# Attention's residual sum on TensorE and ScalarE, its statistics and the fusion moved to other half slots

## The chip, the cores and the metric

The kernel runs on one core of one Trainium2 chip. The metric is the device time of one execution in microseconds; lower is better. All data is float32.

## The reference, cut to what matters

The input is x, 8 samples of 512 channels by 48 x 48 = 2304 positions. Two layers follow, each with its input normalized over groups of 16 channels (`_gn`), and each with its input added to its output.

```
x = x + attention(_gn(x))      # causal linear attention, 8 heads of 64
x = x + mamba4(_gn(x))         # four 128-channel blocks in a chain

attention: q, k, v = 1x1 projections; Q = elu(q)+1; K = elu(k)+1
  out[l] = (sum_{j<=l} (Q[l].K[j]) V[j]) / (Q[l] . sum_{j<=l} K[j])

mamba4, for block i = 0..3:
  x_i = x[:, block i] + fused_{i-1}                 # fused_{-1} = 0
  xs, z = conv and silu of x_i @ Wi;  dt, B, C = xs @ Wx
  h_t = exp(delta_t A) h_{t-1} + delta_t xs_t B_t    # 256 channels x 16 states
  x_m = ((sum_n C_t h_t) + xs D) * silu(z) @ Wo
  fused_i = w_local * x_i + w_global * max(x_i, x_m) # weights from means over positions
```

The layer's output is the four `fused_i`. The statistics of the second `_gn` are taken of the first layer's output, x plus attention.

## The kernel before, in words

**Tiles.** Channels lie on the 128 partitions. The 2304 positions are cut into NC = 6 pieces of LC = 384. A **job** is one piece of one mamba block of one sample: 8 x 4 x 6 = 192 jobs. A **chunk** is one piece of attention for 128 output channels (two heads) of one sample: also 192. Samples are dealt to two streams, and the jobs of both are interleaved by a fixed list of turns; within a stream the jobs follow the chain of blocks.

**Slots and halves.** A job has SLOTS = 8 slots, each with four scans of 128 x 384 (`scan`, L830, on DVE). Order is written out by hand: `slot(k)` issues the product of B and the scaled input for the next slot (`product`, L809, on DVE), the work of other tasks for the first half (`beside(2k)`), two scans, the rest of a product two slots ahead (`last_product`, L798, POOL), the tasks of the second half (`beside(2k + 1)`), and two more scans. Then `weigh` (L846, POOL) multiplies by C, and one slot and a half later `gather` (L853, PE) sums the states into the PSUM tile `yp`. So each job has 16 halves, 0 to 15. Nothing reorders the instructions later: each engine works through its own in the order of issue, and waits by semaphores.

**Decays.** Before each scan ACT computes its decay, exp of 128 x 385 (`decay`, L819), into one of six PSUM banks. Up to three decays are issued ahead (five around the table loads), as far as banks are spare. A scan gives its bank back. All projections and small matmuls take their banks from the same six.

**Tasks.** Chunks, preparations of jobs and the fusion are generators. A `yield` names the half from which the next stage may be issued, and how many banks it needs. A chunk starts at `times[m]`, a multiple of 16 halves plus 3 in most cases. So its stage `at(j)` comes in half (3 + j) mod 16 of a job: the two projections' relu operations in halves 4 and 6, the mask product (L434) in half 8, the output matmuls `ops` (L443, L447, stage 22) in half 9, the sum with the input `xr` (L450, stage 24) and its statistics (L452) in half 11, and in the last chunk of six the group norm's steps from stage 28 on (half 15). The input tile `xr` is loaded anew in stage 18 (L424, half 5); it has one buffer. `save` notes a store, which `flush` issues on SP's queue two halves later or more.

**Preparation of a job** (`prepare`, with `first` the half of its own first scan): the convolution is issued at `first - 21` and `first - 19` (halves 11 and 13; L635), the silu operations with their table loads at `first - 18` (half 14, slot 7; L671 to L676), the copy of dbc (L687) in half 0, and the softplus with its table loads (L706) around half 2; then the two products of delta on POOL (L747), and loads for the scans from `first - 7` on, all on SP's queue.

**Fusion** (`pass_on`) turns the old block's piece in `xi` into the new block's input. For pieces 1 to 5 it loads three tiles (`loads`: xb, fu, xo) at `first - 36`, then from `first - 30` on, half by half, come three ACT operations (L596, L597, L601, in half 2), and three POOL operations: fu (L604), xi (L609) and xo (L612), followed by the store of xo to the output. Piece 0 is done as soon as the block before is finished. The job's convolution reads `xi`; a job may begin when its stream's `ready` exceeds its piece.

Of the kernel before, what the change touches and what calls it, by code (L numbers as in the profile page):

```python
# [49 lines left out]
def attention_then_mamba_kernel(  # L50
# [17 lines left out]
    nc = tc.nc  # L68
    B, _, L = x.shape
# [16 lines left out]
    ident = cst[:, C_ID : C_ID + P]  # L86
# [67 lines left out]
    def save(out, in_):  # L154
        stores.append((half_no[0], out, in_))

    def flush(every=True):
        while stores and (every or stores[0][0] <= half_no[0] - 2):
            _, o, i = stores.pop(0)
            nc.sync.dma_start(out=o, in_=i)  # L160
# [46 lines left out]
    norms, xns, x1s, done, ksums = {}, {}, {}, {}, {}  # L207
# [58 lines left out]
    def chunk(m):  # L266


        b, o, c = parts[m]
        n = f"{b}_{o}_{c}"  # L270
        bank = Banks()
        NT = LC // T
        cols, tile_rows = slice(c * LC, (c + 1) * LC), slice(o * P, (o + 1) * P)
        subs = [slice(i * T, (i + 1) * T) for i in range(NT)]
        heads_of = [slice(par * 64, par * 64 + 64) for par in range(2)]

        def at(j, gap=1):
            return times[m] + j, gap

        def new(tag, bufs=1, shape=(P, LC)):  # L280
            return apool.tile(list(shape), F32, tag=tag, name=f"{tag}_{n}", bufs=bufs)
# [50 lines left out]
        S, stats, ksum = passes[b, o]  # L332
# [9 lines left out]
        q = new("q", 2)  # L342
# [39 lines left out]
        kl, v = new("kl", 1, (P, NT, P)), new("v", 2, (P, NT, P))  # L382
# [20 lines left out]
        place = range(NT + 1) if c % 2 == 0 else range(NT, -1, -1)  # L403
# [19 lines left out]
        xr = new("xr")  # L423
# [8 lines left out]
        for par, sc in enumerate(scs):  # L432
            sm = new(f"sm{par}", 1, (P, NT, T))
# [2 lines left out]
        bank.free(2)  # L436
        yield at(22), 1
        ops = bank()[:, 0:LC]
        for i in range(NT):
            old = c > 0 or i > 0  # L440
            for h, sm in zip(heads_of, sms):
                if old:
                    nc.tensor.matmul(  # L443
                        ops[h, subs[i]], S[h, place[i], :], q[h, subs[i]], start=True, stop=False
                    )
            for h, sm in zip(heads_of, sms):
                nc.tensor.matmul(ops[h, subs[i]], v[:, i, h], sm[:, i, :], start=not old, stop=True)  # L447
        read[0] = m + 1
        yield at(24), 0
        nc.vector.tensor_add(xr, xr, ops)  # L450
        bank.free()
        nc.vector.bn_stats(stats[:, 0, c, :], xr)  # L452
        save(x1s[b][tile_rows, cols], xr)
        if c + 1 == NC:
            norm = yield from group_norm(
                stats, 1, f"m{b}_{o}", 8, [(times[m] + j, 1) for j in (28, 29, 29, 30, 31)]
            )
            flush()
            done[b, o] = norm

    class Stream:
# [62 lines left out]
        def pass_on(self):  # L524


            xi = self.xi
            old = None
            if self.b is not None:
                old = self.b, self.s, self.n, self.fm  # L530
                wt = small.tile([P, 4], F32, tag="wt", name=f"wt_{self.n}")
                nc.vector.tensor_copy(wt[:, 2:3], self.sums)
                nc.vector.tensor_reduce(wt[:, 3:4], self.fsum, AX.X, ALU.add)
            last = old is not None and old[1] == 3 and not self.samples
            if not last:
                self.move_on()
                while (self.b, self.s) not in done:
                    yield "1w", 0
                norm = done[self.b, self.s]
            s = self.s  # L540
            if old is not None:
                yield "1", 0

                nc.scalar.activation(wt[:, 0:2], wt[:, 2:4], AF.Exp, scale=-1.0 / L)
                yield "1", 0
                nc.vector.tensor_scalar_add(wt[:, 0:2], wt[:, 0:2], 1.0)
                nc.vector.reciprocal(wt[:, 0:2], wt[:, 0:2])
            else:
                yield "1", 0
            if not last:  # L550
                if self.fresh:
                    self.sums = norm[:, 2, :]
                else:

                    sums = small.tile([P, 2], F32, tag="sums", name=f"sums_{self.n}", bufs=3)
                    nc.vector.tensor_scalar(
                        sums[:, 0:1], wt[:, 2:3], wt[:, 0:1], norm[:, 2, :], ALU.mult, ALU.add
                    )
                    nc.vector.tensor_scalar(
                        sums[:, 1:2], wt[:, 3:4], wt[:, 1:2], sums[:, 0:1], ALU.mult, ALU.add  # L560
                    )
                    self.sums = sums[:, 1:2]

            def loads(c):
                fu = xb = xa = None
                cols = slice(c * LC, (c + 1) * LC)
                if not last:
                    xb = mpool.tile([P, LC], F32, tag="xb", name=f"xb_{self.n}_{c}")
                    nc.sync.dma_start(out=xb, in_=x1s[self.b][s * P : (s + 1) * P, cols])
                if old is not None:  # L570
                    fu = mpool.tile([P, LC], F32, tag="fu", name=f"fu_{old[2]}_{c}")
                    nc.sync.dma_start(out=fu, in_=old[3][:, cols])
                    xa = mpool.tile([P, LC], F32, tag="xo", name=f"xo_{old[2]}_{c}")
                    nc.sync.dma_start(out=xa, in_=x1s[old[0]][old[1] * P : (old[1] + 1) * P, cols])
                return fu, xb, xa

            now = loads(0)
            for c in range(NC):

                if c and not last:  # L580
                    first = 2 * self.jobs[self.block * NC + c].start
                    yield (first - 36, 1), 0
                    now = loads(c)
                    yield (first - 30, 1), 0
                elif c:
                    yield "3", 0
                    now = loads(c)
                    yield "1", 0
                else:
                    yield "1", 0  # L590
                cols, icols = slice(c * LC, (c + 1) * LC), slice(3 + c * LC, 3 + (c + 1) * LC)
                fu, xb, xa = now
                if not last:
                    normed = dict(bias=norm[:, 1, :], scale=norm[:, 0, :])
                if old is not None:
                    nc.scalar.activation(fu, fu, AF.Copy, scale=wt[:, 1:2])  # L596
                    nc.scalar.activation(xi[:, icols], xi[:, icols], AF.Copy, scale=wt[:, 0:1])  # L597
                if old is None:
                    nc.scalar.activation(xi[:, icols], xb, AF.Identity, **normed)
                elif not last and not self.fresh:  # L600
                    nc.scalar.activation(xb, xb, AF.Identity, **normed)  # L601
                if old is not None:
                    yield "1", 0
                    nc.gpsimd.tensor_tensor(fu, fu, xi[:, icols], ALU.add)  # L604
                    yield "1", 0
                    if not last and self.fresh:
                        nc.scalar.activation(xi[:, icols], xb, AF.Identity, **normed)
                    elif not last:
                        nc.gpsimd.tensor_tensor(xi[:, icols], xb, fu, ALU.add)  # L609
                    self.ready = c + 1  # L610
                    yield "1", 0
                    nc.gpsimd.tensor_tensor(xa, xa, fu, ALU.add)  # L612
                    save(out[old[0], old[1] * P : (old[1] + 1) * P, cols], xa)
                self.ready = c + 1
# [335 lines left out]
    parts, times = [], []  # L950
# [17 lines left out]
    for b in counted:  # L968
        first = times[parts.index((b, 0, 0))]
        begins[b] = (first - 20) // PERIOD * PERIOD - 4 * NC * PERIOD - 2 if b > 1 else first - 64  # L970

    def begin(latest):

        nonlocal begun, put
        while counted and begins[counted[0]] - 4 <= half_no[0]:
            tasks.append(Task(statistics(counted.pop(0))))
        while put < len(parts) and times[put] - 6 <= half_no[0]:
            put += 1
            heads.append(Task(chunk(put - 1), before=heads[-1] if heads else None))
        while (  # L980
            begun < len(jobs)
            and jobs[begun].start <= latest
            and jobs[begun].stream.block == jobs[begun].block
            and jobs[begun].stream.ready > jobs[begun].c
        ):
            tasks.append(Task(jobs[begun].prepare(), jobs[begun].start))
            begun += 1
# [41 lines left out]
    def at(k):  # L1029
        return jobs[k // SLOTS], k % SLOTS  # L1030
# [170 lines left out]
```

## Time and profile before

| | |
|---|---|
| three runs | 9154.76 us median (9140.69 to 9157.51) |
| profiled execution | 9167.14 us |
| its span, first to last instruction | 9165.3 us |
| instructions | 120476 |
| granted TensorE clock, mean | 0.961 |
| busy: DVE, POOL, PE, ACT | 8342.1, 8066.8, 7631.5, 6579.4 us |
| first scan; from the last job's first scan to the end | at 232.2 us; 83.4 us |
| data moved by DMA | 1642.84 MB, mean 179 GB/s; queue 1 takes 65.0% of 16 engines |

How to read it: a line of the groups view gives source line, engine, operation, output from inputs, shape and count, then the group's busy time, the mean duration of one in ns, and the engine's idle time right before its instructions with who ended it. A line of the waits view gives who waited for whom, the total in us, the times and the longest. A line of the timeline gives the start, the duration, engine, line, operation, tiles and how many instructions are merged in it; idle time before the first is in brackets. PE is matmuls and PEld weight loads. A float32 matmul of this kernel appears as two matmul records. Matmul ends are modelled, so PE's busy time is above what the array needs.

### The profile page before, as it was taken

What the parts mean: (1) busy time and instruction counts of PE and PEld (TensorE: products, weight loads), DVE (VectorE), ACT (ScalarE), POOL (GpSimd) and SP (SyncE); (2) the same over time, 40 slices, a digit from 0 to 9 for tenths busy, and PEclk for the clock granted to TensorE, in tenths of its full rate; (3) what the DMA queues carried; (4) which work ended last, traced back from release to release, by engine and by line L of the source; (5) the groups of instructions that cost most, each with busy time, mean ns of one, the idle gap of its engine ahead of it and who ended that gap; (6) DMA issues with size and microseconds to landing.
All of it is one profiled execution on the core that took longest, in us unless ns stands there. A gap on an engine that the chain in (4) does not pass through costs nothing.

```text
span 9165.3 us, 120476 instructions
## 1 busy us (share of the span) xinstructions
PE 7631.5 (83%) x35714; PEld 3602.8 (39%) x35714; DVE 8342.1 (91%) x11640; ACT 6579.4 (72%) x12656; POOL 8066.8 (88%) x5635
## 2 busy tenths in 40 slices
PE   7888888888888888888888888888888888888865
PEld 4443444433344444443333444444333444444321
DVE  3899999999999999999999999999999999999997
ACT  2677777777777777777777777777777777777775
POOL 1788989899988899899998888998999898989998
PEclk9999999999999999999999999999999999999977
DMA  5566666666766666666666666666666666666654
GB/s 182 161 173 180 185 184 184 181 188 180 196 173 179 184 186 187 183 180 181 191 184 182 174 178 187 187 184 184 180 188 183 181 179 177 178 178 177 164 156 129
DMA packets 1002898, 1642.84 MB, mean 179 GB/s; under 512 B 138592, under 2 KB 797312, under 8 KB 1002240
## 3 DMA queue, kind: packets, MB, share of 16 engines
q1 hardware_dynamic: 1002240, 1635.13, 65.0%
q8 instruction: 283, 4.64, 0.2%
q14 instruction: 375, 3.07, 0.1%
HBM read 1309.06 MB, written 325.58 MB: 178 GB/s over the span
## 4 chain that ended last, share of the span: by engine, by line
DVE 31%; ACT 21%; PE 18%; POOL 10%; DMA 9%; issue 8%; SPq 3%; POOLq 0%; DVEq 0%; ACTq 0%
DVE u L830 20%; ACT bank L819 7%; PE bank L635 6%; POOL u L846 6%; DVE u L809 6%; PE bank L286 5%; ACT L819 4%; PE yp L853 3%; PE bank L646 3%; POOL u L798 2%; DMA C<-scr 2%; ACT L706 2%; ACT bank L299 1%; DMA B<-scr 1%; SPq L739 1%
## 5 line engine op out<-in xcount | busy, mean ns | idle before, releaser
L830 DVE TENSOR_TENSOR_SCAN u<-bank,u 128x385 f32<-128x385 f32 (+1 forms) x6144 | 5471.0, 939 | 378.3 <-ACT bank L819 331.9
L846 POOL TENSOR_TENSOR u<-u,C 128x1536 f32<-128x1536 f32 x1536 | 4880.6, 3177 | 216.4 <-DVE gm_m L175 83.2
L819 ACT ACTIVATE bank<-dr,av 128x385 f32<-128x385 f32 (+1 forms) x6144 | 3432.3, 579 | 1406.9 <-DVE u L830 1118.1
L853 PE MATMUL yp<-u,cst 128*64 128x384 f32 x12288 | 2429.2, 516 | 505.7 <-ACT yp L787 263.9
L798 POOL TENSOR_TENSOR u<-B,dxr 128x512 f32<-128x512 f32 x1536 | 1958.8, 1275 | 21.4 <-DMA dxr<-xscr 16.9
L809 DVE TENSOR_TENSOR u<-B,dxp 128x1024 f32<-128x1024 f32 x1536 | 1835.0, 1195 | 9.4 <-ACT dxp L782 9.4
L286 PE MATMUL bank<-xn,wq_sb 128*128 128x384 f32 x4608 | 1730.3, 520 | 97.1 <-DVE u L830 40.4
L853 PEld LDWEIGHTS yp<-u,cst 128*64 128x64 f32 x12288 | 781.0, 139 | 1713.3 <-issue 1051.6
L635 PE MATMUL bank<-xi,wk 128*128 128x384 f32 x3072 | 1122.1, 509 | 306.1 <-ACT kl L383 234.3
L286 PEld LDWEIGHTS bank<-xn,wq_sb 128*128 128x128 f32 x4608 | 870.0, 199 | 894.6 <-DVE u L830 153.6
L635 PEld LDWEIGHTS bank<-xi,wk 128*128 128x128 f32 x3072 | 563.0, 193 | 878.2 <-ACT kl L383 351.5
L844 POOL COPY state<-u 128x4 f32<-128x4 f32 x1280 | 241.7, 189 | 538.4 <-DVE u L830 522.7
L298 ACT ACTIVATE ex<-bank,bqkv_sb 128x384 f32<-128x384 f32 x384 | 219.6, 572 | 520.1 <-PE bank L286 491.6
L747 POOL TENSOR_TENSOR delta<-delta,xs 128x384 f32<-128x384 f32 x384 | 384.6, 1002 | 141.6 <-DMA dscr<-delta 124.6
L819 ACT ACT_TABLE_LOAD x382 | 490.1, 1283 | 6.7
L787 ACT ACTIVATE yp<-xs,pv 128x384 f32<-128x384 f32 x384 | 222.7, 580 | 373.2 <-DVE yz L865 373.2
L871 PE MATMUL bank<-yz,wo 128*128 128x384 f32 x768 | 307.0, 517 | 55.5 <-DVE yz L865 36.7
L695 PE MATMUL bank<-dbc,wd 9*128 9x384 f32 x768 | 302.2, 513 | 3.2 <-ACT dbc L687 3.2
L646 PE MATMUL bank<-xi,wi 128*128 128x384 f32 x768 | 289.2, 498 | 14.3 <-ACT xs L671 14.3
L416 PE MATMUL bank<-cst,rdb 128*128 128x128 f32 x576 | 103.2, 290 | 228.3 <-DVE u L830 226.1
L447 PE MATMUL bank<-sm,v 128*64 128x128 f32 x2304 | 260.9, 305 | 33.8 <-DVE u L830 30.6
L682 PE MATMUL bank<-xs,wx 128*40 128x384 f32 x768 | 281.3, 489 | 0.8 <-DVE sm L434 0.8
(109 smaller groups left out, 7632.7 us busy)
## 6 DMA issues: line engine op xcount, KB each, us to landing
B<-scr SPq DMA_DIRECT2D x1536, 192.0 KB
C<-scr SPq DMA_DIRECT2D x1536, 192.0 KB
xn<-xn SPq DMA_DIRECT2D x192, 768.0 KB
dr<-dscr SPq DMA_DIRECT2D x768, 192.0 KB
dxr<-xscr SPq DMA_DIRECT2D x768, 192.0 KB
dscr<-delta SPq DMA_DIRECT2D x192, 384.0 KB
xscr<-delta SPq DMA_DIRECT2D x192, 384.0 KB
xn<-in_x SPq DMA_DIRECT2D x48, 768.0 KB
```

The lines of the kernel that those rows point to most:

```text
L286: nc.tensor.matmul(ps, wq_sb[:, kt, j * 512 + o * P : j * 512 + (o + 1) * P], xn[:, kt, :], start=(kt == 0), stop=(kt == 3),)
L635: nc.tensor.matmul(xc, wk[:, k, h * P : (h + 1) * P], xi[:, c0 + k : c0 + k + LC], start=(k == 0), stop=(k == 3),)
L646: nc.tensor.matmul(zp, wi[:, 256 + h * P : 256 + (h + 1) * P], xi[:, c0 + 3 : c0 + 3 + LC], start=True, stop=True,)
L695: nc.tensor.matmul(vp, wd[32:41, h * P : (h + 1) * P], dbc[32:41, :], start=True, stop=True)
L747: nc.gpsimd.tensor_tensor(delta[:, h, :], delta[:, h, :], xs[:, h, :], ALU.mult)
L798: nc.gpsimd.tensor_tensor(u[:, :, :, 1 + LC - TAIL :], self.B[s % 4][:, :, cols].unsqueeze(2).to_broadcast(shape), self.dxr[s // 4][:, :, ...
L809: nc.vector.tensor_mul(u[:, :, :, 1 : 1 + LC - TAIL], self.B[s % 4][:, :, cols].unsqueeze(2).to_broadcast(shape), self.dxp.unsqueeze(1).to ...
L819: nc.scalar.activation(dA[:, cols], self.dr[h][:, g, cols], AF.Exp, scale=self.w[6][:, 2 * h + g, q + j : q + j + 1],)
L830: nc.vector.tensor_tensor_scan(u[:, j, g, cols], dA[:, cols], u[:, j, g, cols], 0.0, ALU.mult, ALU.add,)
L846: nc.gpsimd.tensor_tensor(h, h, self.C[s % 4].unsqueeze(2).to_broadcast([P, NG, 2, LC]), ALU.mult)
L853: nc.tensor.matmul(self.yp[g * 64 : g * 64 + 64, 0:LC], pair_sum, u[:, j, g, 1:], start=False, stop=(s % 4 == 3 and j == NG - 1), skip_gro ...
L871: nc.tensor.matmul(self.xm[:, 0:LC], self.w[2][:, h, :], self.yz[:, h, :], start=(h == 0), stop=(h == 1),)
```

## The change

Three things are changed. First, `xr` is put into the bank of `ops` by a matmul with the identity, the attention's own matmuls are added to it in place (none of them starts the bank any more), and ACT copies the bank to `xr`, where DVE added the two. Second, the statistics of `xr` are taken in stage 28 in place of 24, after the store has been noted; the group norm's steps follow with at least one half between them, the last from stage 32. Third, the fusion of pieces 1 to 5 loads at `first - 33` and computes from `first - 25` on. In halves of a job: statistics 11 to 15, fusion's loads 12 to 15, its ACT operations 2 to 7, its POOL operations 3, 4, 5 to 8, 9, 10.

```diff
         ops = bank()[:, 0:LC]
+        nc.tensor.matmul(ops, ident, xr, start=True, stop=False, skip_group_check=True)
         for i in range(NT):
             old = c > 0 or i > 0
             for h, sm in zip(heads_of, sms):
                 if old:
                     nc.tensor.matmul(
-                        ops[h, subs[i]], S[h, place[i], :], q[h, subs[i]], start=True, stop=False
+                        ops[h, subs[i]],
+                        S[h, place[i], :],
+                        q[h, subs[i]],
+                        start=False,
+                        stop=False,
+                        skip_group_check=True,
                     )
             for h, sm in zip(heads_of, sms):
-                nc.tensor.matmul(ops[h, subs[i]], v[:, i, h], sm[:, i, :], start=not old, stop=True)
+                nc.tensor.matmul(
+                    ops[h, subs[i]],
+                    v[:, i, h],
+                    sm[:, i, :],
+                    start=False,
+                    stop=i == NT - 1,
+                    skip_group_check=True,
+                )
         read[0] = m + 1
         yield at(24), 0
-        nc.vector.tensor_add(xr, xr, ops)
+        nc.scalar.copy(xr, ops)
         bank.free()
+        save(x1s[b][tile_rows, cols], xr)
+        yield at(28), 0
         nc.vector.bn_stats(stats[:, 0, c, :], xr)
-        save(x1s[b][tile_rows, cols], xr)
         if c + 1 == NC:
             norm = yield from group_norm(
-                stats, 1, f"m{b}_{o}", 8, [(times[m] + j, 1) for j in (28, 29, 29, 30, 31)]
+                stats, 1, f"m{b}_{o}", 8, [(times[m] + j, 1) for j in (28, 29, 29, 30, 32)]
             )
...
                 if c and not last:
                     first = 2 * self.jobs[self.block * NC + c].start
-                    yield (first - 36, 1), 0
+                    yield (first - 33, 1), 0
                     now = loads(c)
-                    yield (first - 30, 1), 0
+                    yield (first - 25, 1), 0
```

## The prediction

> **What bounds the kernel now.** First the page's busy line:
>
> ```profile
> PE 7631.5 (83%) x35714; PEld 3602.8 (39%) x35714; DVE 8342.1 (91%) x11640; ACT 6579.4 (72%) x12656; POOL 8066.8 (88%) x5635
> ```
>
> DVE is nearest to full, POOL close behind. So ask what fills DVE's other 9%. The waits view (who waited for whom: total, times, longest):
>
> ```profile
> ACT bank L819 <- DVE u L830: 1118.1, 1807, 3.3
> ...
> DVE u L830 <- ACT bank L819: 331.9, 198, 4.4
> ...
> DVE k L351 <- ACT bank L299: 142.0, 135, 5.3
> ...
> DVE norm_m L195 <- POOL norm_m L191: 43.4, 31, 2.2
> ...
> DVE xr L450 <- PE bank L447: 40.2, 16, 8.8
> ```
>
> Most of the time ACT waits for DVE, but 198 times, about once in each of the 192 jobs, a scan waits for its decay, and 135 times k waits for ACT's relu. To place them I counted the scans in the timeline (32 to a job) and laid jobs 12 to 187 over each other: a job takes 46.34 us, of which DVE idles 3.20: 1.58 before the last scan of slot 7, 0.71 before k (slot 3), 0.28 before the norm factors, 0.21 before the first scan of slot 2, 0.09 before the add; the remaining 0.33 is scattered.
>
> The groups view, shapes apart, prices the parts (busy, mean ns, idle before):
>
> ```profile
> L596 ACT ACTIVATE fu<-fu,wt 128x384 f32<-128x384 f32 x192 | 117.0, 609 | 47.8 <-DMA fu<-fm 46.5 <-DVE wt L547 1.2
> ...
> L452 DVE BATCH_NORM_STATS2 stats_m<-xr 128x6 f32<-128x384 f32 x192 | 107.6, 560 | 6.6
> ...
> L450 DVE TENSOR_TENSOR xr<-xr,bank 128x384 f32<-128x384 f32 x192 | 101.4, 528 | 40.2 <-PE bank L447 40.2
> ...
> L384 ACT COPY v<-bank 128x384 f32<-128x384 f32 x192 | 92.8, 483 | 0.0
> ```
>
> Now one job whose first scan starts at 1020.70. ACT's timeline, then PE's, then DVE's:
>
> ```profile
> 1025.19 0.61 ACT L596 ACTIVATE fu<-fu,wt 128x384 f32<-128x384 f32 x1
> 1025.71 0.60 ACT L597 ACTIVATE xi<-xi,wt 128x384 f32<-128x384 f32 x1
> 1026.21 0.69 ACT L601 ACTIVATE xb<-xb,norm_m 128x384 f32<-128x384 f32 x1
> 1026.81 0.57 ACT L819 ACTIVATE bank<-dr,av 128x385 f32<-128x385 f32 x1
> 1027.39 1.28 ACT L706 ACT_TABLE_LOAD   x1
> ...
> 1033.43 0.57 ACT L787 ACTIVATE yp<-xs,pv 128x384 f32<-128x384 f32 x1
> ```
> ```profile
> 1034.15 1.92 PE L853 MATMUL yp<-u,cst 128*64 128x384 f32 x8 [1.99 <-ACT yp L787]
> 1036.00 4.08 PE L286 MATMUL bank<-xn,wq_sb 128*128 128x384 f32 x8
> ```
> ```profile
> 1041.18 0.56 DVE L351 SCALAR_TENSOR_TENSOR k<-ex,bank 128x384 f32<-128x384 f32 x1 [1.89 <-ACT bank L299]
> ```
>
> Fusion stands ahead of the softplus work and its two table loads; the skip into yp comes out late, PE waits 1.99 us for it, its k projection takes 4.08 us (2.85 elsewhere, for example at 1042.32), relu follows, and DVE's k is 1.89 late. The 4.08 is TensorE's clock, as the windows view shows over the same stretch of the job before (mean 1.00, k only 0.15 late) and this one (0.66); PEclk is the third figure from the end:
>
> ```profile
> 988.00:993.50 5.50, 4.64 (x22) 2.43 (x24) 5.50 (x10) 3.57 (x8) 5.50 (x6) 1.00 0.20 71
> 1034.00:1039.00 5.00, 4.85 (x14) 2.32 (x15) 5.00 (x8) 2.64 (x7) 4.92 (x7) 0.66 0.22 84
> ```
>
> The second big stall is the silu slot: from 1061.48 ACT runs a table load, four silus and a load back, and DVE gets its next decay only here:
>
> ```profile
> 1066.78 2.66 DVE L830 TENSOR_TENSOR_SCAN u<-bank,u 128x385 f32<-128x385 f32 x3 [1.11 <-ACT bank L819]
> ```
>
> **What the Trainium skill says.** "TensorE: Matmul & The Clock Gate", Part 1: an idle PE falls to half clock, judged in free-running windows of about 3.4 us. The 0.66 agrees; but its rule of avoiding gaps above some 3 us is too mild here, where 1.99 us was enough (and 1.90 in the job before was not). "ScalarE: Activation LUTs", What ACT_TABLE_LOAD costs: a load is about 1283 ns, and the trace has 1283; the drain of 1380 ns that it adds is not seen (1027.39 + 1.28, next start 1028.69). "PSUM — Partial Sum Buffer", The four PSUM rules: only the first matmul of a group resets a bank, the rest add; so opening the bank with x times identity needs no clearing instruction. No run here shows that yet.
>
> **The change, part by part** (us over the run, negative is a gain).
>
> 1. The add leaves DVE: 192 x 528 ns = -101. DVE is the busiest engine, so it counts in full. Its 40.2 of waits for PE are 16 early ones; in jobs 12 to 187 nearly none at the median: I take 0.
> 2. TensorE gets 192 matmuls of 128x384 by the identity. Eight matmul records (four such products) take 2.85 us, so one is 0.71: +137 on PE, none on the path. PE sits idle 7.35 us per job, among it 1.50 at 1056.58 waiting for pr, right behind the lengthened stretch. It must wait for the load of xr: SP issues that 8.8 us (5th percentile) to 17 us ahead of these matmuls, and loads that something waited for took 2 to 10 us to land. Bounds 0 to +40; I take 0.
> 3. ACT gets 192 copies from PSUM, as `v`: 192 x 483 ns = +93 on ACT, none on the path: behind it in slots 5 to 7 ACT waits 1.87 + 0.72 + 0.25 us per job for DVE before the silu work begins. A late PE would hold up the decays queued behind the copy; three decays ahead (3 x 0.94 us of scans) cover that.
> 4. bn_stats goes from slot 5 to before the third scan of slot 7, inside the silu stall. 560 ns against a mean of 1.58 there (one job in 48 has under 0.56): -107 from slot 5, about +7 where it does not fit: -100. What is late next is the same decay, by 1.0 us instead of 1.58.
> 5. Fusion's three ACT operations (1.9 us of durations, about 1.7 as they overlap) leave half 2 for half 7. Yp comes up to 1.6 us earlier (then the q projection, which ended near 1030.8 in this job, and its two ACT operations set it), PE's pause goes from 1.99 to about 0.4, half clock there becomes rare, and k's wait goes: -142 to 0; I take -110. The first scan of slot 2 waits for a decay behind the second table load, 0.21 x 176 = 37: I take -25. In half 7 ACT waited 0.53 + 0.27 + 0.80 us for DVE afterwards, which takes in most of 1.7: 0 to +30, I take 0.
> 6. Fusion's POOL operations (3 x 1.0) go from halves 3, 4, 5, where they stood against the two delta products (2 x 1.0, halves 5, 6), to 8, 9, 10. POOL's start of `weigh` lags the scans by 2.35 us at the median in slot 2 and 5.5 at the 95th percentile; that shrinks. Its three loads move on SP from half 12 to 15, with 8 halves to use instead of 6, behind B2 and C0 and ahead of B3 of the next job; the out store moves from before xscr to before B2, and SP now waits for it there. SP waited 1277 us for dbc and 968 for delta, so it has slack: 0.
> 7. The group norm's steps come one half later, and POOL's power then no longer stands right before DVE's use: -43 to 0, I take -20.
>
> Sum: -101 - 100 - 110 - 25 - 20 = -356. Against it stands POOL. In a stretch with the xn scaling it is busy 529 of 569 us (12 jobs), 44.1 per job, and some 16 handoffs of 0.07 make 45.2. DVE alone would come to 46.34 - 1.85 = 44.5 on average. I give back 60. So -296: 9167 - 296 = 8871 for the profiled execution, which stood 12 above the median; 9154.8 - 296 = 8859, put at **8860**. Its own range is 8800 to 8950.
>
> **Rivals.**
> - The burst moves instead of going. If fusion at half 7 starves slot 4 as it starved slots 2 and 3, parts 5 and 7 bring nothing: -201 + 60 gives about -140 to -200, some 8985. For it: ACT's 1.7 us is a little more than the idle time there. Against: no table load stands beside it.
> - POOL becomes the bound early. On average 42.8 busy + 1.1 of handoffs + 0.6 waiting for delta's store = 44.5, with local crowding 45.0: 1.3 x 192 = 250, some 8905, and 8940 if lag also blocks u.
> - Slower: conv waits for fusion. xi is now written at half 9 on POOL, conv reads it at half 11. After slot 3's last scan POOL needs lag + 3.2 (weigh) + 1.0 + 1.28 + 1.0; conv starts 8.34 after it at the median. With the lag of 0.33 it is 1.5 us in time; with 5.9 (95th percentile of before) 4 us late. A late conv delays silu and so the stall in slot 7, once 1.5 us of cover (the wait for pr) is used. It decides from about 3.4 us of mean lateness (cover and the gain of 1.9); 4.5 us on 168 chunks would be +185: 9340. Against it: the lag shrinks by part 6.
>
> **Numbers.** Main case 0.57, moved burst 0.20, POOL 0.15, conv 0.06, all cancelling 0.02. A measurement tells about 0.2% (18 us; the three runs spread 17). Faster 0.92, same 0.02, slower 0.06. The range 8760 to 9040 takes in the first three cases and the bounds of parts 5 to 7.
>
> **What would show it.** Right: L830's wait for L819 falls from 331.9 to about 230; k's wait under 40; the clock in the stretch after the skip near 1.00; DVE's busy time about 100 less; conv's waits for xi still the few at block starts. Wrong: new scan waits in slot 4, POOL above 95% with waits of DVE on L798's products, or conv waiting for xi in every job.

## The result, and the profile after

| | before | changed |
|---|---|---|
| median of the runs | 9151.35 us (4 runs, 9140.69 to 9157.51) | 8984.74 us (4 runs, 8978.6 to 8990.42) |
| profiled execution / its span | 9167.14 / 9165.3 us | 8983.06 / 8981.0 us |
| granted TensorE clock, mean | 0.961 | 0.959 |

The ratio is 0.982, 95% interval [0.9805, 0.9835]: 167 us faster. The direction was forecast and the time lies in the range, but the forecast gain was 296, and the question is where the other 129 us went.

The busy line of the changed kernel's page:

```profile
PE 7759.3 (86%) x36098; PEld 3681.5 (41%) x36098; DVE 8252.1 (92%) x11448; ACT 6629.5 (74%) x12848; POOL 8058.8 (90%) x5635
```

DVE has lost 90.0 us of work and PE has gained 127.8; POOL does nearly the same work (8066.8 before) in less time. The waits view of the changed kernel, DVE's rows (who waited for whom, total, times, longest). L844 is the scan (L830 before), L879 reads yp:

```profile
DVE u L844 <- ACT bank L833: 253.5, 187, 4.6
DVE q L343 <- ACT bank L299: 145.5, 66, 6.0
DVE stats_a L239 <- DMA xs<-in_x: 54.2, 34, 3.7
DVE yz L879 <- PE yp L867: 42.3, 29, 5.0
...
DVE k L351 <- ACT bank L299: 29.6, 62, 3.1
```

The two rows the prediction was after have shrunk: the scan's wait from 331.9 to 253.5, k's from 142.0 to 29.6. But the wait of q, the step just before k, has grown to 145.5; this is its row before:

```profile
DVE q L343 <- ACT bank L299: 36.3, 16, 6.0
```

The waits of yz and stats_a have grown too. Three rows of the groups view show the pieces that were moved, with their prices: the identity product (two records to a product), the copy, the statistics:

```profile
L439 PE MATMUL bank<-xr,cst 128*128 128x384 f32 x384 | 186.0, 568 | 64.9 <-DVE u L844 64.3 <-ACT kl L383 0.5
...
L467 DVE BATCH_NORM_STATS2 stats_m<-xr 128x6 f32<-128x384 f32 x192 | 105.6, 550 | 0.0
...
L463 ACT COPY xr<-bank 128x384 f32<-128x384 f32 x192 | 90.3, 470 | 58.5 <-PE bank L453 39.7 <-issue 18.8
```

To see which jobs got the gain, I counted the scans in the timeline again and took the mean length of jobs 12 to 185 by the remainder of the job's number modulo six, called its place here (the two streams are interleaved, so a place is not a piece of one block). Place 0 holds the loads of the next stage's weights, place 2 the second of the group norm's two small products (L186):

| place | 0 | 1 | 2 | 3 | 4 | 5 |
|---|---|---|---|---|---|---|
| before, us per job | 46.63 | 46.02 | 48.13 | 46.02 | 45.50 | 46.12 |
| changed | 46.84 | 45.59 | 48.61 | 43.72 | 44.62 | 43.45 |

Places 3 and 5 gained 2.3 and 2.7 us, more than the forecast mean of 1.5 per job (296 / 192). Places 0 and 2 even lost a little, and place 1 gained 0.4. So two causes were to be found: one in place 2, one in places 0 and 1. Place 4 gained 0.9; the runs below that mend the other places leave it at 44.6 to 44.7, and it was not followed up.

**Place 2.** PE's timeline in such a job of the changed kernel (first scan at 1130.26):

```profile
1130.63 0.38 PE L171 MATMUL bank<-mv_m,cst 128*128 128x1 f32 x2
...
1137.59 0.59 PE L186 MATMUL bank<-gm_m,cst 128*128 128x1 f32 x2 [3.65 <-ACT delta L720]
...
1141.56 3.75 PE L286 MATMUL bank<-xn,wq_sb 128*128 128x384 f32 x8
```

L171 and L186 are the group norm's two small products. The second needs a PSUM bank, and by the wait it is handed the one from which ACT reads the softplus's input (L720). PE stands 3.65 us, and the q projection behind it runs at 3.75 us instead of 2.85. PEclk (third from the end in the windows view) is 0.93 over this job, and DVE waits 2.33 us for q's input. The waits view of before has no row of L186 waiting for softplus; in the changed kernel PE waits for it 30 times, 108.8 us in all (the weight loads of the same products show the same pauses again). The Trainium skill ("TensorE: Matmul & The Clock Gate", Part 1), which the prediction cited, has an idle PE fall to half clock, and the trace agrees: PEclk is 1.00 for the first 2.8 us of this pause and 0.50 for the 6.83 us after them.

**Places 0 and 1.** The windows view of the changed kernel, a job of place 0 and the one after it (POOL's busy time is the fifth figure after the width, PEclk the third from the end):

```profile
1039.90:1085.10 45.20, 39.33 (x197) 19.02 (x198) 42.71 (x59) 35.96 (x72) 39.80 (x30) 1.00 0.72 195
1085.20:1130.20 45.00, 40.02 (x185) 19.19 (x182) 42.80 (x59) 33.88 (x69) 43.91 (x26) 0.96 0.72 197
```

POOL loses 5.4 us in the first and has only 1.1 to spare in the second, where it works off its arrears and two of PE's gathers wait for `weigh`, 3.0 us in all. What it waits for stands in POOL's rows of the waits view, changed kernel first, then before:

```profile
POOL delta L761 <- DMA dscr<-delta: 191.0, 93, 23.2
```
```profile
POOL delta L747 <- DMA dscr<-delta: 124.6, 33, 21.6
```

### The profile page after: what moved, and what is told of

Its sections match the earlier page's. It is cut to its first block, busy times and chain, and to the rows that moved or that the text cites. A ratio compares the mean times of both kernels' runs of the same rounds, so it can differ in the third digit from the quotient of the medians.

```text
span 8981.0 us, 121595 instructions
## 1 busy us (share of the span) xinstructions
PE 7759.3 (86%) x36098; PEld 3681.5 (41%) x36098; DVE 8252.1 (92%) x11448; ACT 6629.5 (74%) x12848; POOL 8058.8 (90%) x5635
## 4 chain that ended last, share of the span: by engine, by line
DVE 37%; POOL 13%; PE 13%; ACT 13%; DMA 11%; issue 8%; SPq 4%; POOLq 0%; DVEq 0%; ACTq 0%
DVE u L844 23%; POOL u L860 8%; DVE u L823 7%; ACT bank L833 4%; PE bank L286 4%; PE yp L867 3%; SPq L753 3%; PE bank L649 3%; DMA C<-scr 2%; POOL u L812 2%; ACT L833 2%; ACT L720 2%; DMA dscr<-delta 1%; DVE yz L879 1%; DMA xo<-x 1%
## 5 line engine op out<-in xcount | busy, mean ns | idle before, releaser
L844 DVE TENSOR_TENSOR_SCAN u<-bank,u 128x385 f32<-128x385 f32 (+1 forms) x6144 | 5449.4, 937 | 273.8 <-ACT bank L833 253.5
L867 PE MATMUL yp<-u,cst 128*64 128x384 f32 x12288 | 2471.0, 524 | 389.7 <-POOL u L860 313.1
L286 PE MATMUL bank<-xn,wq_sb 128*128 128x384 f32 x4608 | 1681.1, 508 | 88.3 <-POOL xn L310 33.2
L649 PE MATMUL bank<-xi,wk 128*128 128x384 f32 x3072 | 1104.1, 502 | 274.3 <-ACT kl L383 184.1
```

Of the source, the lines that this page charges most:

```text
L286: nc.tensor.matmul(ps, wq_sb[:, kt, j * 512 + o * P : j * 512 + (o + 1) * P], xn[:, kt, :], start=(kt == 0), stop=(kt == 3),)
L649: nc.tensor.matmul(xc, wk[:, k, h * P : (h + 1) * P], xi[:, c0 + k : c0 + k + LC], start=(k == 0), stop=(k == 3),)
L844: nc.vector.tensor_tensor_scan(u[:, j, g, cols], dA[:, cols], u[:, j, g, cols], 0.0, ALU.mult, ALU.add,)
L867: nc.tensor.matmul(self.yp[g * 64 : g * 64 + 64, 0:LC], pair_sum, u[:, j, g, 1:], start=False, stop=(s % 4 == 3 and j == NG - 1), skip_gro ...
```

## The experiments

Each series was timed together with the kernel before on one chip, but the three series were on three chips. Where a gain or loss in us is given without more, it is the difference of the medians to the kernel before of the same series (9155.65, 9151.71 or 9156.05). A difference between runs of two series is that of their medians, and since these three differ by up to 4.3 us, it is uncertain by about as much. In the expectations, theory 1 is the norm's bank (place 2), and theory 3 is SP's queue with the wait of POOL that it causes (places 0 and 1).

| label | what it is | median us | ratio to before, 95% |
|---|---|---|---|
| e2_fusion_only | before, fusion moved | 9089.08 | 0.9926 [0.9912, 0.9941] |
| e3_sum_only | before, sum on PE and ACT | 9119.86 | 0.9960 [0.9945, 0.9975] |
| e4_stats_only | before, statistics moved | 9064.76 | 0.9902 [0.9885, 0.9918] |
| e6_norm_late | before, norm's steps later | 9169.34 | 1.0021 [1.0014, 1.0028] |
| e9_before_weights | before, weights behind dscr | 9131.73 | 0.9976 [0.9966, 0.9985] |
| e11_fusion_weights | before, fusion moved, weights behind dscr | 8988.64 | 0.9818 [0.9803, 0.9832] |
| e1_norm_early | changed, norm's steps early | 8958.08 | 0.9782 [0.9768, 0.9797] |
| e5_store_late | e1, out store later | 8957.20 | 0.9787 [0.9773, 0.9802] |
| e7_weights_after | e1, weights behind dscr | 8845.28 | 0.9663 [0.9647, 0.9680] |
| e8_both | e5 and e7 | 8837.46 | 0.9656 [0.9642, 0.9671] |
| e10_after_weights | changed, weights behind dscr | 8864.27 | 0.9683 [0.9668, 0.9697] |
| e12_sum_stats | e1, fusion where it was before | 8968.32 | 0.9796 [0.9782, 0.9811] |

### First series: the change taken apart

**e1_norm_early**: the changed kernel, with the norm's first step allowed in the half of the statistics, so that both its banks are taken earlier.

```diff
-                stats, 1, f"m{b}_{o}", 8, [(times[m] + j, 1) for j in (28, 29, 29, 30, 32)]
+                stats, 1, f"m{b}_{o}", 8, [(times[m] + j, gap) for j, gap in ((28, 0), (29, 1), (29, 1), (30, 1), (32, 1))]
```

> The changed kernel, with the group norm's first step in the same half as the last statistics, so that its five steps stand in halves 28 to 32 as before the change, and not 29 to 33. Theory 1 (the norm's bank): the second norm matmul (L186) took a bank that softplus had still to read, and TensorE stood 3.65 us in 32 jobs behind it, which made those jobs 49 us long; here the bank comes from elsewhere, the wait of L186 for ACT goes, these jobs come to 44 to 46 us, and the whole to 8985 - 32 x 4 = about 8860 (8830 to 8900). Rival 2 (POOL and SP's queue set the rest): the wait only changes its name, and the time stays within 20 us of 8985.

Measured: 8958.08, 27 below the changed kernel. L186's wait for softplus is gone from the trace, q's wait fell from 145.5 to 91.4, and place 2 went from 48.61 to 47.66. The mechanism is right, its size is not: the forecast was about 8860, with these jobs at 44 to 46 us, and it explains 27 us, not the whole shortfall. Part of it is given back, since the norm factors are needed sooner and wait for POOL again (53.9, against 8.0 in the changed kernel).

**e2_fusion_only**: the kernel before with the fusion's two times of the changed one.

```diff
-                    yield (first - 36, 1), 0
+                    yield (first - 33, 1), 0
...
-                    yield (first - 30, 1), 0
+                    yield (first - 25, 1), 0
```

> The kernel before with only fusion's loads and operations moved (first - 33, first - 25). By the prediction's parts 5 and 6: k's wait from 142 to under 40, the scan behind the second table load on time, so 9151 - 110 - 25 = about 9016 (8980 to 9050). Rival 2: the output store now stands before the next job's B rows on SP and POOL is close to full, and half of this is given back: 9085.

Measured: 9089.08, a gain of 67, where part 5 had 135. K's wait went as forecast (142.0 to 30.9), so the forecast gain was made and half of it lost elsewhere: q's wait rose to 90.9. The time is the rival's number, 9085; its reason, the output store's place on SP's queue, is tried in e5. In this kernel nothing of the norm was touched, so the shortfall has a second cause, and the fusion's move brings it in.

**e3_sum_only**: the kernel before with the identity product, the added matmuls and ACT's copy; the statistics stay right behind the sum.

```diff
+        nc.tensor.matmul(ops, ident, xr, start=True, stop=False, skip_group_check=True)
...
-        nc.vector.tensor_add(xr, xr, ops)
+        nc.scalar.copy(xr, ops)
```

> The kernel before with only the sum moved to TensorE and ScalarE; statistics stay right behind the copy, fusion where it was. By the prediction's parts 1 to 3: DVE 101 us less busy, nothing else late: 9050 (9030 to 9080). Rival 2: DVE waits for the copy or a late TensorE makes the silu work late, and the gain is under 40: 9120.

Measured: 9119.86, a gain of 36, the rival's number. This row of its waits view takes back most of the 101 us of the add:

```profile
DVE stats_m L465 <- ACT xr L463: 114.2, 189, 8.5
```

In nearly every chunk DVE reaches the statistics before ACT's copy is done. The sum alone is worth little; it needs the statistics to stand later.

**e4_stats_only**: the kernel before with the statistics, and the norm's places, of the changed one.

```diff
-        nc.vector.bn_stats(stats[:, 0, c, :], xr)
         save(x1s[b][tile_rows, cols], xr)
+        yield at(28), 0
+        nc.vector.bn_stats(stats[:, 0, c, :], xr)
...
-                stats, 1, f"m{b}_{o}", 8, [(times[m] + j, 1) for j in (28, 29, 29, 30, 31)]
+                stats, 1, f"m{b}_{o}", 8, [(times[m] + j, 1) for j in (28, 29, 29, 30, 32)]
```

> The kernel before with only the statistics moved into the silu slot and the norm steps that follow, as in the changed kernel. Prediction's part 4 and 7: 9151 - 100 - 20 = 9030. Theory 1: the statistics bring the 100, but the norm's bank costs 32 waits of TensorE of about 3.7 us, of which 2 to 3.5 us reach the scans: -100 + 65 to 110, so 9115 to 9160, with L186's wait for ACT at about 115 us.

Measured: 9064.76, a gain of 91. Theory 1's 9115 to 9160 missed: it put the cost of the norm's bank at 65 to 110, too high here as in e1. The scan's wait falls from 331.9 to 244.3, so the statistics hide in the silu stall; q's wait rises to 93.6, most of which e6 below shows to be the norm's share (81.7 there).

### Second series: the second cause

In a job of place 0 SP issues nine loads of weights and only then the store of delta to dscr. The first product of delta on POOL overwrites delta, so it must wait for that store, and everything behind it on POOL waits too. POOL's timeline in e1_norm_early (first scan of the job at 1043.38):

```profile
1056.16 1.28 POOL L812 TENSOR_TENSOR u<-B,dxr 128x512 f32<-128x512 f32 x1
1062.87 1.00 POOL L761 TENSOR_TENSOR delta<-delta,xs 128x384 f32<-128x384 f32 x1 [5.43 <-DMA dscr<-delta]
1063.81 0.19 POOL L858 COPY state<-u 128x4 f32<-128x4 f32 x1
```

SP's timeline there, first and last load of the weights and the store:

```profile
1050.55 0.54 SPq L493 DMA_DIRECT2D wi<-in_win  x1
...
1058.72 0.42 SPq L510 DMA_DIRECT2D av<-in_alog  x1
1059.94 0.38 SPq L729 DMA_DIRECT2D dscr<-delta  x1
```

The store is issued 9.4 us behind the first load; 3.6 of them SP waits, ahead of the fourth load, for the load of xn. Before, the same queue had the same order; the POOL timeline of the kernel before in the same job:

```profile
1077.06 1.00 POOL L604 TENSOR_TENSOR fu<-fu,xi 128x384 f32<-128x384 f32 x1
...
1081.41 0.99 POOL L609 TENSOR_TENSOR xi<-xb,fu 128x384 f32<-128x384 f32 x1
...
1083.59 0.99 POOL L612 TENSOR_TENSOR xo<-xo,fu 128x384 f32<-128x384 f32 x1
1086.80 1.00 POOL L747 TENSOR_TENSOR delta<-delta,xs 128x384 f32<-128x384 f32 x1 [2.22 <-DMA dscr<-delta]
```

The fusion's three operations, 3 us of work, stood ahead of the delta product, and so the wait was 2.22. With these three behind it, as in e1, it is 5.43. "Perfetto Trace Analysis" of the Trainium skill (Tensor Engine Instruction (MATMUL, LD_WEIGHTS)) states that ACT, DVE and GPSIMD take their instructions strictly in order. The trace agrees: the state copy at 1063.81 comes right behind the product, with no wait of its own, though the scans whose states it copies ended on DVE at 1058.70, and `weigh` comes behind that. To test the cause, e7 puts the store ahead of the weights; two other suspects, the store of xo on SP and the norm's place by itself, were tried with it.

**e5_store_late**: e1 with a pause ahead of `save` of xo to the output, so that SP does not wait for POOL's xo ahead of the load of a later slot's B rows (B2 in the prediction).

```diff
+                    yield "2", 0
                     save(out[old[0], old[1] * P : (old[1] + 1) * P, cols], xa)
```

> The kernel of e1 with the store of fusion's output noted two halves later, so that it no longer stands on SP's queue right ahead of the load that the input statistics (L239) need. Theory 3: the 59 us that L239 waits for its load go, and some of it reaches the end: 8958 - 30 to 60, about 8915. Rival: the waits sit beside stalls of the silu slot, and nothing changes: 8958 +- 15.

Measured: 8957.20, nothing beside e1's 8958.08. SP's wait for xo falls from 953.5 to 275.8 us and L239's for its load from 58.6 to 28.1, as the edit meant, and no time comes of it: the rival's case.

**e6_norm_late**: the kernel before with the norm's steps one half later.

```diff
-                stats, 1, f"m{b}_{o}", 8, [(times[m] + j, 1) for j in (28, 29, 29, 30, 31)]
+                stats, 1, f"m{b}_{o}", 8, [(times[m] + j, 1) for j in (29, 30, 30, 31, 32)]
```

> The kernel before with only the group norm's five steps one half later each, as the change has them. Theory 1 as e1 left it: L186 waits about 115 us for ACT's softplus and q gains some 50 us of waits, while DVE's wait for the norm's power (43 us) goes: 9156 + 5 to 40, about 9175. Without the bank's effect it would be 9156 - 20 to 40.

Measured: 9169.34, 18 slower. PE's wait for softplus appears with nothing else changed:

```profile
PEld bank L186 <- ACT delta L706: 124.7, 30, 4.3
PE bank L186 <- ACT delta L706: 106.2, 30, 3.7
```

Part 7, taken as a gain of 20, is a loss of 18.

**e7_weights_after**: e1 with the weights' loads created behind the store.

```diff
-            if c == NC - 1 and (st.s < 3 or st.samples):
-                tasks.append(Task(st.weights()))
...
             dsrc = spread("dscr")
+            if c == NC - 1 and (st.s < 3 or st.samples):
+                tasks.append(Task(st.weights()))
```

> The kernel of e1 with one step moved on SP's queue: the loads of the next block's weights, in one job of six, are issued behind the store of delta (dscr) and not ahead of it. Theory 3 (SP's queue): in these jobs the weight loads hold up the store, POOL's first product of delta waits 5.4 us for it in the open (before the change fusion's POOL work stood ahead of that product and covered it), POOL is then late to the end of the job and into the next, gathers wait for it, and q's relu with them. So POOL's wait for dscr falls from 191 to under 70 us, q's wait on DVE from 91 to under 45, and the time from 8958 by 60 to 120: 8840 to 8900. Rival 2 (POOL is simply full): the idle time turns up elsewhere on POOL and the time stays within 20 of 8958.

Measured: 8845.28, 113 below e1. In jobs of place 0 the idle time before POOL's first delta product falls from 5.02 to 0.77 us at the mean of 30; places 0 and 1 go from 46.67 and 45.67 to 44.15 and 44.32, the other places stay within 0.11. (2.52 + 1.35) x 30 = 116, close to the gain. Two signs came only in part. The total of the waits view falls less than expected (252.1 to 147.8, not below 70): what is left is the start of the run, 22.1 in one wait, and short waits in other jobs, which were there in e1 too. And q's wait falls from 91.4 to 67.1, not below 45. A job of place 0 in e7: SP's store and first load, then POOL's first delta product, which no longer waits:

```profile
1045.83 0.51 SPq L726 DMA_DIRECT2D dscr<-delta  x1
1046.44 0.53 SPq L493 DMA_DIRECT2D wi<-in_win  x1
...
1052.70 1.00 POOL L760 TENSOR_TENSOR delta<-delta,xs 128x384 f32<-128x384 f32 x1
```

The windows view of e7, this job and the next:

```profile
1038.60:1082.00 43.40, 39.08 (x190) 18.54 (x190) 42.65 (x59) 34.73 (x70) 42.24 (x31) 1.00 0.80 218
1082.00:1125.70 43.70, 39.50 (x193) 18.96 (x194) 43.12 (x63) 35.20 (x71) 41.94 (x26) 1.00 0.71 193
```

POOL's lost 5.4 us are down to 1.2, and the clock of the second job is back from 0.96 to 1.00.

**e8_both**: e7 with e5's pause; its edits are those two diffs.

> Both of these on top of e1. Theory 3: the two add up, 8958 - 90 - 40 = about 8830 (8790 to 8880). Rival 2: POOL at 8060 us of work cannot be fed faster, and it stays above 8920.

Measured: 8837.46, 314 below before. Next to e7 the pause brings about 8, where 40 were expected, with intervals of the ratio that overlap (0.9663 [0.9647, 0.9680] and 0.9656 [0.9642, 0.9671]); e7's runs lie from 8840.83 to 8846.08, these from 8835.02 to 8840.12. A small gain is likely, and its cause was not looked for.

### Third series: what each part is worth with the cover restored

**e9_before_weights, e10_after_weights, e11_fusion_weights**: the edit of e7, as shown there, made in the kernel before, in the changed kernel, and in e2.

> The kernel before with one edit: the loads of the next stage's weights are issued on SP behind the delta store of dscr instead of ahead of it. Theory 3 (the fusion's POOL operations stood ahead of the delta products and covered the wait for dscr in the kernel before; only moving them away uncovered it): before has only about 2.2 us of POOL idle left in such a job, some 31 jobs, and part of it is hidden: -20 to -60, about 9115. Rival (the weights' place costs by itself, whatever the fusion does): the same as the 113 measured with the changed kernel, about 9040.

Measured: 9131.73, a gain of 24. Before, POOL idled 2.56 us ahead of the delta product in place 0; with the edit nothing is left of it, and place 0 goes from 46.63 to 45.55. The same edit that is worth 113 in e1 is worth 24 here. That excludes that the weights' place costs 113 by itself, whatever the fusion does.

> The changed kernel as it is, with the norm's late steps, and only the weights' loads moved behind the store of dscr. If the two losses (SP's order; the group norm's bank) simply add: 8985 - 113 = about 8870 (8860 to 8885). If the norm's late bank takes more once POOL is on time, 8890 to 8910; if it is hidden then, 8850.

Measured: 8864.27, 120 below the changed kernel. The two causes add: the norm's late bank is what separates it from e7 (19 us, across two series whose intervals overlap; place 2 takes 48.52 against 47.55).

> The kernel before with the fusion five halves later and the weights' loads behind the store of dscr. Theory 3: the fusion's move is worth what the prediction's part 5 said once the delta product no longer waits: 9152 - 135 = about 9016 (8990 to 9040). Rival: the move alone is worth only the 67 it brought by itself, with the weights' own gain of some 20 to 40 added: 9045 to 9070.

Measured: 8988.64. Against e9 the fusion's move is now worth 143; without the weights' edit it was worth 67 (e2). Part 5 had forecast 135. K's wait is 21.8 and q's is 49.5, down from 90.9 in e2.

**e12_sum_stats**: e1 with the fusion's two times of before.

```diff
-                    yield (first - 33, 1), 0
+                    yield (first - 36, 1), 0
...
-                    yield (first - 25, 1), 0
+                    yield (first - 30, 1), 0
```

> The changed kernel with the norm's steps early and the fusion where it was before (sum by TensorE and ScalarE, statistics in the silu slot, nothing else). Theory: the 101 of the add, which the sum alone lost to a new wait of its statistics for ScalarE's copy (114), shows once the statistics stand four halves later: 9152 - 101 - 91 = about 8960 (8945 to 8985). Rival: the parts only add as measured alone (-32 and -87, and -27 for the norm's steps early): 9005 to 9035.

Measured: 8968.32, a gain of 188, where parts 1 and 4 together had 201. Alone, the sum (36) and the statistics (91, with the norm's loss of 18 in it) come to 145. The 114.2 of e3 is gone: with the statistics four halves later, the waits view has no row left of DVE waiting for ACT's copy.

## Why the prediction was right in direction and wrong in size

By its own steps:

- **Part 1, the add (-101), and part 4, the statistics (-100): right together.** e12 shows 188. DVE's busy time fell by 90.0 (8342.1 to 8252.1), forecast about 100. What the text did not say: part 1 rests on part 4. e3 alone shows most of the add's time turned into a wait for the copy.
- **Parts 2 and 3, PE and ACT at 0: no cost seen once the statistics stand later.** The identity products take 186.0 us of PE (568 ns a record) instead of the estimated 137, and the copies 90.3 (93 forecast). None of L439's waits is for the load of xr. That the first matmul of a bank needs no clearing instruction ("PSUM — Partial Sum Buffer", The four PSUM rules) fits: the kernel issues 384 more matmul records, all of them L439, and no other instruction for it.
- **Part 5, ACT's fusion operations (-135): right.** PE's wait for the skip, before and changed:

```profile
PE yp L853 <- ACT yp L787: 263.9, 164, 5.0
```
```profile
PE yp L867 <- ACT yp L801: 74.3, 174, 3.8
```

K's wait fell from 142.0 to 29.6, DVE's idle time before the first scan of slot 2 from 0.21 us a job to 0.00, and e11 against e9 measures 143.
- **Part 6, SP and POOL at 0: this is the step that failed.** It argued from SP's total of waits, an average over all jobs ("so it has slack"), and moved 3 us of POOL work from ahead of the delta products to behind them without asking what these products wait for. The prediction had the wait in hand, as an average: its POOL rival counts 0.6 us a job "waiting for delta's store" (124.6 / 192). In one job of six they wait for a store behind nine loads of weights, and the moved work had covered it. It costs 113 to 120 in the changed kernel (e1 to e7, changed to e10), of which 24 were there before (e9): 89 to 96 by the move itself. The view that shows it was at hand: L747's wait for dscr, 124.6 in 33 times, is about one in six jobs.
- **Part 7, the norm (-20): wrong sign.** Norm_m's wait for POOL went as forecast (43.4 to 8.0), but one half later the bank for L186 is the one that softplus reads. e6 measures +18, e1 27, e10 against e7 19. The step priced the wait that goes and not the bank that each matmul asks for. This is the second step that failed.
- **The give-back to POOL (+60): near in size, its reason mostly not borne out.** The 60 had no working. Sum and statistics (188), fusion on top of the weights' order (143) and that order (24) come to 355; e7, which has all three, gains 306. So 49 are given back. The job lengths place them: over half lies outside the jobs with the xn scaling, 0.2 us in each of 138 jobs. There k's wait counts twice: of its 0.84 us a job before, e12 takes 0.18 and e11 0.83, and e7 can save it only once (0.01 left). The rest lies in the 36 jobs with the xn scaling (37 to 48, 85 to 96, 133 to 144). They take 47.30 us before and 47.31 in e7, so the change gains nothing there, against 46.17 and 43.94 in the others. The fusion's move alone makes them longer, from 46.74 (e9) to 47.26 (e11). In e7 DVE stands idle 4.56 us in such a job, 0.90 of it before q. POOL is busy 43.9 of the 47.3, so it is not full there either; what makes q late in these jobs was not tried on its own.

Parts 6 and 7 together: about 120 + 19 = 139 measured between the changed kernel and e7, against the 129 that were missing. With SP's order alone mended, e10 stands at 8864.27, beside the forecast of 8860. Part of that agreement is chance, since e10 has the norm's loss in it and takes the old 24 away.

**The rivals.** The moved burst gave 8985, which is the time measured, by another mechanism: DVE stands idle 0.00 us a job before the scans of slot 4, and k's wait was nearly gone. A new wait, before the second scan of slot 5, is only 0.17 us a job, and 0.06 in e7. POOL as the bound: the 42.8 us a job that the prediction took for its work adds durations that overlap, and POOL was busy 41.9; in the changed kernel it is 90% busy, under the 95% set, and most of its lateness came from one wait in one job of six, since mending that wait brought 113 to 120. Conv waiting for xi: 59 waits of 80.9 us by PE's matmuls (24 of 54.8 before), more than the few at block starts, but far from one per job. **What would show it** came true for k (under 40), for the scan's wait in direction (253.5, forecast about 230; 245.6 in e10) and for DVE. The mean clock did not rise (0.961 to 0.959). Of the trace's half-clock records, those around the skip (13 to 17 us into the job) went from 47 to 6, but those 5 to 9 us into the job rose from 23 to 55, 30 of them in place 2, where L186 waits; e7 has 31 and a mean of 0.974.

## What to carry to other kernels

Work that is moved away from a place may have been covering a wait there: before pricing a move at nothing, look at the instruction that stood behind it on the same engine, at what it waits for, and at that transfer's place in its queue, in the job where the queue is fullest rather than on average. A queue's total of waits doesn't tell its slack at one place. If a change is made of several moves, a gain may need two of them together (the sum needed its statistics elsewhere), and a step that takes a bank or buffer later may be handed one that is still in use.

## What the runs showed of the hardware

- A TensorE pause well under 3 us can halve its clock, but near 2 us its length alone does not decide. The prediction took from one pair that 1.99 us was enough and 1.90 was not. Over the whole trace of the kernel before, of the pauses of 1.80 to 1.95 us 1 of 25 was followed by half clock within 3.4 us, of those of 1.95 to 2.10 us 38 of 67, of those above 3 us 26 of 27.
- In these traces the stretches at half clock begin at whole multiples of 3.413 us from one another. If the trace of the kernel before is cut into windows at these times, each of the 53 full-clock windows in which PE was busy under 1.4 us was followed by half clock, and 19 of the 1,936 in which it was busy 2 us or more. PE's ends are modelled, so 1.4 is rough. The records at half clock number 136 in the kernel before, 711.7 us in all (mean 5.2 us), 120 in the changed one (743.4) and 81 in e7 (457.0).
- A float32 product of 128x384 by the identity shows as two records of 568 ns at the mean in this stream, of modelled ends, and 186.0 / 192 = 0.97 us of busy PE; the copy of its bank by ACT takes 470 ns, near the 483 ns of the copy of v.
